# Layer 1's attention of a two-layer Perceiver: weights made key-major instead of query-major

## The chip, the cores and the metric

The kernel runs on one NeuronCore of a Trainium2 chip. The core has five instruction queues that run side by side and meet through semaphores: TensorE (PE in the profile, with PEld for its weight loads), VectorE (DVE), ScalarE (ACT), GpSimd (POOL) and SyncE (SP), which issues most of the DMAs. The metric is the device time of one execution in microseconds. Before the change it was 2016.11 us, the median of three runs (2011.85 to 2018.19).

## The reference, cut to what matters

A batch of 64 sequences of 32 tokens (2048 rows of 256 channels) passes two layers. Layer 0: attention over a context of 257 rows a sequence, an RWKV-like mixing with a feed-forward part, and a mixture of eight experts of which two are used. Layer 1: a second attention over the same context, a Mamba-like state-space recurrence, and a dense mixture of eight experts. Each part is added to the residual stream `x`.

The change lies in layer 1's attention alone. Queries, keys and values come from projections with ternary weights on quantised rows (the quantised context is kept in DRAM and is common to both). There are 16 query heads and 8 key/value heads of 16 channels; two query heads share a key head. For each sequence, head and query:

```python
w = softmax(q @ k.T)          # over 257 keys
o = w @ v                     # then a layer norm, a quantised output projection, and x + o
```

The softmax is computed as exponentials of the score less the row's maximum, divided by their sum.

## The kernel before, in words

The rows are worked in four blocks of 512 (16 sequences); a tile is 128 rows, four sequences, so there are 16 tiles. `_stage0` to `_stage5` build the two layers, and `layers` (L1294) writes them in program order, interleaving calls: layer-1 attention `s3` runs in slices of units while other stages' blocks are called between them. The order on each engine's queue is not that order by itself: the framework's scheduler places instructions by its own estimates, so the work of several stages is mixed on each queue, and each queue then runs strictly in the placed order.

A unit, `step` (L732), is two of a tile's four sequences. There are 32, two a tile. The work of a unit is spread over two steps: in the first, `keys` (L854) makes `kT` (PE L859, DVE L861) and `v` (PE L866, four ACT copies L874), and `scores` (L876), once for each pair of key heads, makes 128 queries x 256 keys of scores for two sequences in two PSUM banks (L882), their maxima on DVE (L887, joined with the score of the 257th key at L889), and eight exponentials a unit on ACT (L893), each with a sum along the row. In the next step `sums` (L898) turns these weights with 16 PE transposes (L911), copies them out on ACT (L913), multiplies them with the values (L919), and combines the two key heads that share a lane (ACT L924, DVE L925). After a tile's second unit `back` (L927) forms the reciprocals, brings them to the layout of the output with a small matmul, transposes the output, scales it, and adds the part of the 257th key (L931 to L967). After every second tile `finish` (L768) norms and quantises, and one step later projects and adds to `x` (L798).

`attend` (L802) opens a tile: it loads the quantised context and its steps, and makes the queries twice masked by `half` in `qm` (L840), the 257th key `klm` (L831) and value `vr` (L827), and the scores of that key (L843).

PSUM: pool `ps` has two banks with one tag; scores, `pt_ps` and more go through them. `pk` takes the one bank of `psp` where `k.lent` is set, else `ps`; while `k.idle` is set, `oT_ps` takes the bank of `psu`.

What follows from a block of layer-1 attention: `ahead` (L1023) norms `x` of a finished block, projects, convolves and makes the step sizes; then `recur` (L1087) begins with `dtx` (L1096) and runs 64 scans on DVE (L1110, with a product at L1111), each fed by an ACT exponential (L1109) and POOL products (L1105, L1116). After it come `head` and the experts of `_stage5` (L1265, L1273), a long run of 512-column matmuls.

## Time and profile before

| | |
|---|---|
| median of three runs | 2016.11 us |
| profiled execution, first to last instruction (span) | 2007.7 us; the profile gives no other time of it |
| median less span | 8.4 us |
| units 0 to 8 (start of unit 0's `kT` to unit 9's) | 490.9 to 779.6 us |
| recurrence 0, `dtx` and scans | 775.6, 780.9 to 998 us |
| recurrence 1 | 1088.2, 1096.8 to 1336 us |
| recurrence 2 | 1389.3, 1399.1 to 1635 us |
| last unit's combine (L925) | 1551.7 us |
| recurrence 3 | 1654.8, 1667 to 1843 us |
| the experts' rest, PE alone | 1843 to 2004 us |

How to read it. Each engine's share is a mean over stages with different limits, so a stretch is read by its own busy times. Busy PE time includes the pipelined end of each matmul, so PE that is busy all the time is not at its peak rate; how far matmuls are apart is read from their start times. "DVE L925" means a VectorE instruction of source line 925. In groups of instructions, the numbers after the bar are total busy us, mean ns of one, then idle us of the engine just ahead of these and what ended most of it.

### The profile page before, as it was taken

What the parts mean: (1) busy time and instruction counts of PE and PEld (TensorE: products, weight loads), DVE (VectorE), ACT (ScalarE), POOL (GpSimd) and SP (SyncE); (2) the same over time, 40 slices, a digit from 0 to 9 for tenths busy, and PEclk for the clock granted to TensorE, in tenths of its full rate; (3) what the DMA queues carried; (4) which work ended last, traced back from release to release, by engine and by line L of the source; (5) the groups of instructions that cost most, each with busy time, mean ns of one, the idle gap of its engine ahead of it and who ended that gap; (6) DMA issues with size and microseconds to landing.
All of it is one profiled execution on the core that took longest, in us unless ns stands there. A gap on an engine that the chain in (4) does not pass through costs nothing. (4 is left out here: it accounts for less than half of the span.)

```text
span 2007.7 us, 20180 instructions
## 1 busy us (share of the span) xinstructions
PE 1550.7 (77%) x6323; PEld 803.3 (40%) x6323; DVE 1272.7 (63%) x2207; ACT 999.6 (50%) x2172; POOL 1105.5 (55%) x1369
## 2 busy tenths in 40 slices
PE   4765966749988978766777878679878576898998
PEld 2333533424644633433443434334434233334443
DVE  4578477376385257988954778665768564876300
ACT  2453353121553436545537657548757454675432
POOL 5444655433134234777862578764678756998000
PEclk9686876769998989777787778779879796899999
DMA  7654324030000101222201223201313120442221
GB/s 228 218 182 146 119 94 127 26 102 0 22 22 22 53 11 59 64 53 64 74 11 49 64 52 106 74 32 49 106 42 85 59 63 21 125 126 64 74 84 42
DMA packets 88378, 151.25 MB, mean 75 GB/s; under 512 B 7740, under 2 KB 52300, under 8 KB 86224
## 3 DMA queue, kind: packets, MB, share of 16 engines
q1 hardware_dynamic: 85428, 148.75, 24.4%
q10 hardware_dynamic: 2844, 1.22, 0.3%
q8 instruction: 50, 0.82, 0.2%
q14 instruction: 56, 0.46, 0.1%
HBM read 139.03 MB, written 10.92 MB: 75 GB/s over the span
## 5 line engine op out<-in xcount | busy, mean ns | idle before, releaser
L1105 POOL TENSOR_TENSOR g<-dtx,bc 128x1024 f32<-128x1024 f32 x128 | 301.6, 2358 | 128.2 <-DVE h L1110 85.1
L1110 DVE TENSOR_TENSOR_SCAN h<-h,g 128x512 f32<-128x512 f32 x256 | 307.9, 1219 | 62.7 <-ACT h L1109 61.9
L1116 POOL TENSOR_TENSOR xc<-xc,hc 128x1024 f32<-128x1024 f32 x128 | 301.8, 2359 | 33.1 <-DVE hc L1111 26.7
L1265 PE MATMUL up<-xT,w 128*128 128x512 f32 x512 | 273.6, 655 | 20.5 <-ACT hid L1267 19.6
L1273 PE MATMUL acc<-hid,w 128*128 128x512 f32 x512 | 262.2, 637 | 28.4 <-ACT hid L1269 28.4
L1109 ACT ACTIVATE h<-dt,A 128x512 f32<-128x512 f32 x256 | 173.5, 693 | 98.9 <-DVE hc L1111 98.4
L1111 DVE TENSOR_TENSOR hc<-h,bc 128x512 f32<-128x512 f32 x256 | 170.8, 681 | 3.5
L893 ACT ACTIVATE p<-sc,nm 128x256 f32<-128x256 f32 x256 | 117.7, 471 | 111.1 <-DVE nm L889 100.3
L1273 PEld LDWEIGHTS acc<-hid,w 128*128 128x128 f32 x512 | 100.6, 205 | 148.1 <-issue 104.2
L1267 ACT ACTIVATE hid<-up,chan 128x512 f32<-128x512 f32 x128 | 86.7, 683 | 136.8 <-PE up L1265 136.6
L630 PE MATMUL weps<-we,xT 128*128 128x512 f32 x256 | 139.6, 672 | 19.2 <-DVE x L632 14.2
L1265 PEld LDWEIGHTS up<-xT,w 128*128 128x128 f32 x512 | 100.0, 207 | 132.9 <-issue 92.6
L882 PE MATMUL sc<-kT,qm 32*128 32x256 f32 x512 | 118.2, 449 | 7.4 <-ACT p L893 2.4
L911 PE MATMUL pt_ps<-ident,p 128*128 128x128 f32 x512 | 92.1, 315 | 30.1 <-ACT p L893 29.9
L887 DVE TENSOR_REDUCE nm<-sc 128x2 f32<-128x512 f32 x128 | 84.1, 684 | 28.2 <-PE sc L882 27.3
L911 PEld LDWEIGHTS pt_ps<-ident,p 128*128 128x128 f32 x512 | 64.8, 158 | 70.9 <-ACT p L893 48.9
L913 ACT COPY pt<-pt_ps 128x512 f32<-128x512 f32 x128 | 72.6, 586 | 38.9 <-PE pt_ps L911 31.4
L247 POOL TENSOR_TENSOR cT<-cT,scb 128x2056 f32<-128x2056 f32 x16 | 74.5, 4654 | 29.8 <-PE sc L258 11.1
L882 PEld LDWEIGHTS sc<-kT,qm 32*128 32x128 f32 x512 | 69.0, 205 | 45.7 <-issue 17.0
L1020 PE MATMUL inps<-xT,w_L_attn_in_projT 128*128 128x512 f32 x128 | 70.8, 679 | 20.6 <-ACT zs L1085 15.5
L919 PE MATMUL oT_ps<-pt,v 128*32 128x128 f32 x1024 | 68.8, 302 | 21.5 <-ACT pt L913 21.0
L530 POOL TENSOR_TENSOR kk<-kk 128x512 f32<-128x512 f32 x32 | 34.2, 1073 | 92.7 <-ACT kk L529 92.7
(407 smaller groups left out, 3032.7 us busy)
## 6 DMA issues: line engine op xcount, KB each, us to landing
bc<-rows SPq DMA_DIRECT2D x64, 512.0 KB
w<-in_L_ffn_w_dram SPq DMA_DIRECT2D x64, 512.0 KB
cT<-in_ctxT_dram SPq DMA_DIRECT2D x16, 1028.0 KB
cq<-cq SPq DMA_DIRECT2D x32, 514.0 KB
cn<-in_ctx_dram SPq DMA_DIRECT2D x64, 256.0 KB
scb<-scales SPq DMA_DIRECT2D x16, 514.0 KB
kb<-steps SPq DMA_DIRECT2D x16, 514.0 KB
x<-in_x_dram SPq DMA_DIRECT2D x4, 512.0 KB
```

The source lines that it names most:

```text
L630: nc.tensor.matmul(ps, xT[:, c, r], we[:, c, e : e + 2, :], start=c == 0, stop=c == 1)
L882: nc.tensor.matmul(sc[h][:, f, :], qm[r, e + f].rearrange("p l n g -> p (l n g)"), kTs[e][r, f, :], start=True, stop=True,)
L893: nc.scalar.activation(w_[:, f, h - h0, :], sc[h][:, f, :], AF.Exp, bias=nm[:, e + f, h : h + 1], accum_out=sm[:, e + f, h : h + 1],)
L911: nc.tensor.transpose(pt_ps[:, h, m, :], ws[e, hp][:, f, h, m * P : (m + 1) * P], k.ident)
L1105: nc.gpsimd.tensor_tensor(g, dtx[:, c2 : c2 + 2], bc[:, 0:1, :].to_broadcast([P, 2, BT]), ALU.mult)
L1109: nc.scalar.activation(h, dt, AF.Exp, scale=A[:, c2 + c, n : n + 1])
L1110: nc.vector.tensor_tensor_scan(h, h, g[:, c, :], 0.0, ALU.mult, ALU.add)
L1111: nc.vector.tensor_tensor(hc[:, c, :], h, bc[:, 1, :], ALU.mult)
L1116: nc.gpsimd.tensor_tensor(y[:, c2 : c2 + 2], y[:, c2 : c2 + 2], hc, ALU.add)
L1265: nc.tensor.matmul(u, w1[e][:, c, q * P : (q + 1) * P], xT[:, c, :], start=c == 0, stop=c == 1)
L1267: nc.scalar.activation(hid[e][:, q, :], u, AF.Identity, bias=b1)
L1273: nc.tensor.matmul(acc[o], w2[e][:, q, o * P : (o + 1) * P], hid[e][:, q, :], start=n == H, stop=n == E * H + H - 1)
```

## The change

The weights are made with keys along the partitions, the layout that the product with the values takes; the transposes of the weights go.

`tops` is the former `scores` without exponentials: the natural scores are made for their maxima only, and the negated maxima are written into a fixed tile `nmx`. `turn` transposes that tile once a unit (`nmT`), and makes the weights of the 257th key in turned form (`plT`). `weights`, in the next step, fills a PSUM bank a head with the negated maxima (a matmul that picks the row of the head and sequence and repeats it over all keys), adds keys times queries to it, and takes one exponential of 128x512 a head. `sums` multiplies with values laid out beside columns of ones (`vm`, `vls`), so that each product brings its weights' sum along with it; `back` transposes four 128x128 blocks, takes the reciprocals of the sums and multiplies. `values` is split from `keys` and moved to the end of the step, `qm` gets a second buffer, and the 257th key's values are made for 16 rows from a repeated copy on POOL (`ends4`). The scores are therefore computed twice, once in each layout.

```diff
--- before
+++ after
@@ -322,7 +323,8 @@

         of(dql, aml, ssl, "l")
         nc.scalar.dma_start(k.steps[:, :, 2 * P : S].rearrange("g e o -> (g e) o"), dql)
-        nc.sync.dma_start(k.dql, k.steps[:, :, 2 * P : S].rearrange("g e o -> e (g o)"))
+        for h in range(4):
+            nc.sync.dma_start(k.dql[4 * h : 4 * h + 4], k.steps[:, :, 2 * P : S].rearrange("g e o -> e (g o)"))
         cdq = k.cdq.rearrange("p t g -> p (t g)")
         of(cdq, am.rearrange("p t g -> p (t g)"), ss.rearrange("p t g -> p (t g)"), "s")
         dT_ps = pb.tile([P, P], F32, name="dT_ps", tag="b")
@@ -681,14 +683,40 @@
     half = w.tile([P, 2], F32, name="half", tag="half")
     nc.vector.tensor_reduce(half, k.ident.rearrange("p (i l d) -> p l i d", l=2, d=16), AX.XY, ALU.add)

-    sel = w.tile([P, T], F32, name="sel", tag="sel")
-    nc.vector.tensor_reduce(sel, k.ident.rearrange("p (l n g) -> p n l g", l=2, g=2), AX.XY, ALU.add)
-    lgm = w.tile([P, 2, 2], F32, name="lgm", tag="lgm")
-    nc.vector.tensor_reduce(lgm, k.ident.rearrange("p (l n g) -> p l g n", l=2, g=2), AX.X, ALU.add)
-    lgm = lgm.rearrange("p l g -> p (l g)")
-
...
+    three = w.tile([P, 3], F32, name="three", tag="three")
+    nc.vector.tensor_reduce(three, k.ident.rearrange("p (h r) -> p r h", r=32)[:, 0:3], AX.X, ALU.add)
+    pick = w.tile([P, 2, P], F32, name="pick", tag="pick")
+    nc.vector.tensor_copy(pick, three[:, 0:2].unsqueeze(2).to_broadcast([P, 2, P]))
+    pickl = w.tile([P, 4, 4, 4], F32, name="pickl", tag="pickl")
+    for e in range(4):
+        for at in range(4):
+            r = e % 2 if at == e else 2
+            nc.vector.tensor_scalar(pickl[:, e, :, at], k.bmask, three[:, r : r + 1], None, ALU.mult)
+
...
+    def fixed(name, shape, fill, rows=P):
+        t = k.wk3.tile([rows, *shape], F32, name=name, tag=name, bufs=1)
+        nc.gpsimd.memset(t, fill)
+        return t
+
+    nmxs = [fixed(f"nmx{n}", [4, 32], 0.0) for n in range(2)]
+    for nmx in nmxs:
+        nc.gpsimd.memset(nmx[:, :, 2:3], NONE)
+    klxs = [fixed(f"klx{n}", [68], 0.0) for n in range(2)]
+    vm = fixed("vm", [2, 2, 4, 2, 2, 16], 1.0)
+    vls = [k.wk3.tile([16, 2, 4, 2, 16], F32, name=f"vl{n}", tag=f"vl{n}", bufs=1) for n in range(2)]
+    for vl in vls:
+        nc.vector.tensor_copy(vl[:, :, :, 1, :], own.unsqueeze(1).unsqueeze(3).to_broadcast([16, 2, 4, 16]))
+    cdq = w.tile([P, 8, NT], F32, name="cdq3", tag="cdq3")
+    nc.vector.tensor_scalar(cdq, k.cdq, mw[:, 2:3], None, ALU.mult)
+    dql1 = w.tile([16, NT], F32, name="dql1", tag="dql1")
+    nc.vector.tensor_scalar(dql1, k.dql, mw[0:16, 2:3], None, ALU.mult)
+    dql = w.tile([16, NT, 4], F32, name="dql3", tag="dql3")
+    nc.vector.tensor_tensor(
+        dql, own.unsqueeze(1).to_broadcast([16, NT, 4]), dql1.unsqueeze(2).to_broadcast([16, NT, 4]), ALU.mult,
+    )

...
@@ -742,12 +770,19 @@
                 h = halves[t // 2]
                 tiles[t] = attend(t, t % 2, h.xq, h.dq, h.o4)
             tiles[t].keys(e)
-            tiles[t].scores(e, 0)
+            tiles[t].tops(e, 0)
         if old:
             lt, le = divmod(2 * u - 2, 4)
+            tiles[lt].weights(le, 0)
+        if new:
+            tiles[t].tops(e, 2)
+        if old:
+            tiles[lt].weights(le, 2)
+        if old:
             tiles[lt].sums(le)
         if new:
-            tiles[t].scores(e, 2)
+            tiles[t].turn(e)
+            tiles[t].values(e)
         if old and le == 2:
             tiles[lt].back()
             if lt % 2:
@@ -819,37 +854,46 @@
         nc.scalar.activation(q, q_ps, AF.Copy, scale=dq[:, j : j + 1])

         last_ps = pk([P, P + 4], "last_ps")
+        ends4 = k.small.tile([P, 2, 4, 4], BF16, name="ends4", tag="ends4")
         for c in range(2):
-            nc.tensor.matmul(last_ps[0:4, 0:P], cq[:, c, :, 2 * P], wkv[:, c, P : 2 * P], start=c == 0, stop=c == 1)
+            nc.gpsimd.tensor_copy(ends4[:, c], cq[:, c, :, 2 * P].unsqueeze(1).to_broadcast([P, 4, 4]))
+        for c in range(2):
+            nc.tensor.matmul(
+                last_ps[0:16, 0:P], ends4[:, c].rearrange("p h e -> p (h e)"), wkv[:, c, P : 2 * P],
+                start=c == 0, stop=c == 1,
+            )
         for c in range(2):
             nc.tensor.matmul(last_ps[:, P : P + 4], wkv[:, c, 0:P], cq[:, c, :, 2 * P], start=c == 0, stop=c == 1)
-        vr = k.wk3.tile([4, P], F32, name="vr", tag="vr")
-        nc.scalar.activation(vr, last_ps[0:4, 0:P], AF.Copy, scale=k.dql[:, g : g + 1])
+        klx, vl = klxs[g % 2], vls[g % 2]
+        nc.vector.tensor_tensor(
+            vl[:, :, :, 0, :], last_ps[0:16, 0:P].rearrange("p (h l d) -> p l h d", l=2, d=16),
+            dql[:, g].unsqueeze(1).unsqueeze(3).to_broadcast([16, 2, 4, 16]), ALU.mult,
+        )
         kl = last_ps[:, P : P + 4]
         nc.vector.tensor_tensor(kl, kl, kb[:, :, 2 * P], ALU.mult)
-        klm = k.small.tile([P, 4, 4], F32, name="klm", tag="klm")
         nc.vector.tensor_tensor(
-            klm, kl.unsqueeze(2).to_broadcast([P, 4, 4]), k.bmask.unsqueeze(1).to_broadcast([P, 4, 4]), ALU.mult
+            klx.rearrange("p (e q) -> p e q", q=17)[:, :, 0:16].rearrange("p e (h m) -> p e h m", m=4)[:, :, :, 0],
+            kl.unsqueeze(2).to_broadcast([P, 4, 4]), k.bmask.unsqueeze(1).to_broadcast([P, 4, 4]), ALU.mult,
         )
+        klx = klx[:, 0:64].rearrange("p (e h m) -> p e h m", h=4, m=4)
...
-        qm = k.wk3.tile([P, 4, 2, T, 2], F32, name="qm", tag="qm", bufs=1)
+        qm = k.wk3.tile([P, 4, 2, T, 2], F32, name="qm", tag="qm")
         for l in range(2):
             nc.scalar.activation(qm[:, :, l].rearrange("p e n g -> p g e n"), qT_ps, AF.Copy, scale=half[:, l : l + 1])
         sl_ps = pk([P, 4, 4], "sl_ps")
         for e in range(4):
-            nc.tensor.matmul(sl_ps[:, e, :], qm[:, e].rearrange("p l n g -> p (l n g)"), klm[:, e, :], start=True, stop=True)
+            nc.tensor.matmul(sl_ps[:, e, :], qm[:, e].rearrange("p l n g -> p (l n g)"), klx[:, e, :, e], start=True, stop=True)
         nsl = k.small.tile([P, 4, 4], F32, name="nsl", tag="nsl")
         nc.scalar.activation(nsl, sl_ps, AF.Copy, scale=-1.0)

...
@@ -859,6 +903,8 @@
                 nc.tensor.matmul(kT_ps, wkv[:, c, 0:P], cq[:, c, e : e + 2, 0 : 2 * P], start=c == 0, stop=c == 1)
             kTs[e] = k.wk3.tile([P, 2, 2 * P], F32, name="kT", tag="kT")
             nc.vector.tensor_tensor(kTs[e], kT_ps, kb[:, e : e + 2, 0 : 2 * P], ALU.mult)
+        def values(e):
+
             v_ps = pk([P, 2, 2, P], "v_ps")
             for m in range(2):
                 for f in range(2):
@@ -867,13 +913,15 @@
                             v_ps[:, m, f, :], cq[:, c, e + f, m * P : (m + 1) * P], wkv[:, c, P : 2 * P],
                             start=c == 0, stop=c == 1,
                         )
-            vs[e] = k.wk3.tile([P, 2, 2, P], F32, name="v", tag="v")
-            cd = k.cdq[:, :, g].rearrange("p (m e) -> p m e", m=2)[:, :, e : e + 2]
+            cd = cdq[:, :, g].rearrange("p (m e) -> p m e", m=2)[:, :, e : e + 2]
             for m in range(2):
                 for f in range(2):
-                    nc.scalar.activation(vs[e][:, m, f, :], v_ps[:, m, f, :], AF.Copy, scale=cd[:, m, f : f + 1])
-
-        def scores(e, h0):
+                    nc.scalar.activation(
+                        vm[:, m, f, :, :, 0, :], v_ps[:, m, f, :].rearrange("p (h l d) -> p h l d", l=2, d=16),
+                        AF.Copy, scale=cd[:, m, f : f + 1],
+                    )
+
+        def tops(e, h0):
             hs = range(h0, h0 + 2)
             sc = {h: ps([P, 2, 2 * P], "sc") for h in hs}
             for f in range(2):
@@ -885,15 +933,49 @@
                     )
             for h in hs:
                 nc.vector.tensor_reduce(nm[:, e : e + 2, h], sc[h], AX.X, ALU.max, negate=True)
-            n2 = nm[:, e : e + 2, h0 : h0 + 2]
-            nc.vector.tensor_tensor(n2, n2, nsl[:, e : e + 2, h0 : h0 + 2], ALU.min)
-            w_ = ws[e, h0 // 2] = k.wk3.tile([P, 2, 2, 2 * P], F32, name="p", tag="p", bufs=3)
+            nmx[e] = nmxs[(2 * g + e // 2) % 2]
+            nc.vector.tensor_tensor(
+                nmx[e][:, h0 : h0 + 2, 0:2].rearrange("p h f -> p f h"),
+                nm[:, e : e + 2, h0 : h0 + 2], nsl[:, e : e + 2, h0 : h0 + 2], ALU.min,
+            )
+
+        def turn(e):
+
+            nl_ps = pk([P, 3, P], "nl_ps")
+            nc.tensor.transpose(nl_ps[:, 2, :], nmx[e].rearrange("p h r -> p (h r)"), k.ident)
+            nmT[e] = k.wk3.tile([P, P], F32, name="nmT", tag="nmT", bufs=1)
+            nc.scalar.copy(nmT[e], nl_ps[:, 2, :])
+            for f in range(2):
+                o = nl_ps[0:16, f, :]
+                nc.tensor.matmul(o, pickl[:, e + f].rearrange("p h m -> p (h m)"), nmT[e], start=True, stop=False)
+                nc.tensor.matmul(
+                    o, klx[:, e + f].rearrange("p h m -> p (h m)"), qm[:, e + f].rearrange("p l n g -> p (l n g)"),
+                    start=False, stop=True,
+                )
+            plT[e] = k.wk3.tile([16, 2, P], F32, name="plT", tag="plT", bufs=1)
+            nc.scalar.activation(plT[e], nl_ps[0:16, 0:2, :], AF.Exp)
+
+        def weights(e, h0):
+            hs = range(h0, h0 + 2)
+            sT = {h: ps([P, 2, 2, P], "sT") for h in hs}
+            for f in range(2):
+                for h in hs:
+                    r = slice(32 * h, 32 * h + 32)
+                    nc.tensor.matmul(
+                        sT[h][:, f], pick[r, f, :], nmT[e][r, :].unsqueeze(1).to_broadcast([32, 2, P]),
+                        start=f == 0, stop=False, skip_group_check=True,
+                    )
+            for f in range(2):
+                for m in range(2):
+                    for h in hs:
+                        r = slice(32 * h, 32 * h + 32)
+                        nc.tensor.matmul(
+                            sT[h][:, f, m, :], kTs[e][r, f, m * P : (m + 1) * P],
+                            qm[r, e + f].rearrange("p l n g -> p (l n g)"), start=False, stop=True, skip_group_check=True,
+                        )
             for h in hs:
-                for f in range(2):
-                    nc.scalar.activation(
-                        w_[:, f, h - h0, :], sc[h][:, f, :], AF.Exp, bias=nm[:, e + f, h : h + 1],
-                        accum_out=sm[:, e + f, h : h + 1],
-                    )
+                ws[e, h] = k.wk3.tile([P, 2, 2, P], F32, name="p", tag="p", bufs=4)
+                nc.scalar.activation(ws[e, h], sT[h], AF.Exp)

         def sums(e):

@@ -902,71 +984,38 @@
             else:
                 oT_ps = pk([P, 2, 2, 2 * T], "oT_ps")
             for f in range(2):
-                pts = []
-                for hp in range(2):
-
-                    pt_ps = ps([P, 2, 2, P], "pt_ps")
-                    for h in range(2):
-                        for m in range(2):
-                            nc.tensor.transpose(pt_ps[:, h, m, :], ws[e, hp][:, f, h, m * P : (m + 1) * P], k.ident)
-                    pt = k.wk3.tile([P, 2, 2, P], F32, name="pt", tag="pt")
-                    nc.scalar.copy(pt, pt_ps)
-                    pts.append(pt)
-                ob = oT_ps[:, f].rearrange("p l q -> p (l q)")
+                for l in range(2):
+                    nc.tensor.matmul(
+                        oT_ps[:, f, l, :], vls[g % 2][:, l].rearrange("p h w d -> p (h w d)"),
+                        plT[e][:, f, l * 2 * T : (l + 1) * 2 * T], start=f == 0 and l == 0, stop=False, skip_group_check=True,
+                    )
+            for f in range(2):
                 for m in range(2):
-                    for h in range(4):
-                        r = slice(32 * h, 32 * h + 32)
-                        nc.tensor.matmul(
-                            ob[r], vs[e][:, m, f, r], pts[h // 2][:, h % 2, m, :],
-                            start=m == 0, stop=m == 1, skip_group_check=True,
-                        )
-            o2 = od4[:, e : e + 2]
-            nc.scalar.activation(o2, oT_ps[:, :, 0], AF.Copy, scale=half[:, 0:1])
-            nc.vector.scalar_tensor_tensor(o2, oT_ps[:, :, 1], half[:, 1:2], o2, ALU.mult, ALU.add)
+                    for l in range(2):
+                        for h in range(4):
+                            nc.tensor.matmul(
+                                oT_ps[32 * h : 32 * h + 32, f, l, :], vm[:, m, f, h, l].rearrange("p w d -> p (w d)"),
+                                ws[e, h][:, f, m, l * 2 * T : (l + 1) * 2 * T], start=False, stop=m == 1, skip_group_check=True,
+                            )
+            nc.scalar.copy(
+                od.rearrange("p l (e n) g -> p e l (n g)", e=4)[:, e : e + 2], oT_ps,
+            )

         def back():

-            rp = k.small.tile([P, 2, 4, 4], F32, name="rp", tag="rp3", bufs=1)
-            rs, pl = rp[:, 0], rp[:, 1]
-            nc.vector.tensor_tensor(pl, nm, nsl, ALU.subtract)
-            nc.scalar.activation(pl, pl, AF.Exp)
-            nc.vector.tensor_tensor(sm, sm, pl, ALU.add)
-            nc.vector.reciprocal(rs, sm)
-            nc.vector.tensor_tensor(pl, pl, rs, ALU.mult)
-
...
-            o = o4[:, j].rearrange("p i l g d -> p g (i l) d")
-            nc.vector.tensor_tensor(o, po_ps, over(0), ALU.mult)
...
-            nc.gpsimd.tensor_tensor(o, o, t, ALU.add)
-
-        a.keys, a.scores, a.sums, a.back = keys, scores, sums, back
+
+        a.keys, a.values, a.tops, a.turn, a.weights, a.sums, a.back = keys, values, tops, turn, weights, sums, back
         return a

     return run
```

## The prediction

> **What bounds the kernel now.** I read the page first, then the busy time of each engine stretch by stretch, cut at the starts of units (a unit is one step of the layer-1 attention, two of a tile's four sequences; there are 32).
>
> ```profile
> span 2007.7 us, 20180 instructions
> PE 1550.7 (77%) x6323; PEld 803.3 (40%) x6323; DVE 1272.7 (63%) x2207; ACT 999.6 (50%) x2172; POOL 1105.5 (55%) x1369
> ...
> L893 ACT ACTIVATE p<-sc,nm 128x256 f32<-128x256 f32 x256 | 117.7, 471 | 111.1 <-DVE nm L889 100.3
> ...
> L911 PE MATMUL pt_ps<-ident,p 128*128 128x128 f32 x512 | 92.1, 315 | 30.1 <-ACT p L893 29.9
> L887 DVE TENSOR_REDUCE nm<-sc 128x2 f32<-128x512 f32 x128 | 84.1, 684 | 28.2 <-PE sc L882 27.3
> ...
> L913 ACT COPY pt<-pt_ps 128x512 f32<-128x512 f32 x128 | 72.6, 586 | 38.9 <-PE pt_ps L911 31.4
> ...
> L919 PE MATMUL oT_ps<-pt,v 128*32 128x128 f32 x1024 | 68.8, 302 | 21.5 <-ACT pt L913 21.0
> ```
>
> No engine is full over the span; the groups that change wait for one another in a ring, DVE maxima, ACT exponentials, PE transposes, ACT copies, PE sums. Which wait costs depends on the stretch (time of units 0-8, 9-13, 14-18, 19-23, 24-26, 27-31):
>
> ```profile
> 490.90:779.60 288.70, 256.88 (x1234) 145.12 (x1232) 152.00 (x349) 141.05 (x354) 89.45 (x209) 0.92 0.09 27
> 779.60:933.70 154.10, 107.67 (x560) 59.85 (x559) 141.44 (x234) 78.22 (x208) 117.79 (x112) 0.77 0.20 55
> 933.70:1075.90 142.20, 107.83 (x570) 56.83 (x569) 104.73 (x205) 73.95 (x193) 89.69 (x153) 0.83 0.15 47
> 1075.90:1250.00 174.10, 136.80 (x600) 70.73 (x601) 127.16 (x196) 114.39 (x246) 114.49 (x97) 0.79 0.26 72
> 1250.00:1404.50 154.50, 122.34 (x472) 60.09 (x472) 95.93 (x148) 96.15 (x176) 99.51 (x126) 0.86 0.18 56
> 1404.50:1552.00 147.50, 117.96 (x632) 62.65 (x629) 118.58 (x190) 97.39 (x227) 109.64 (x95) 0.87 0.26 76
> ```
>
> After start, end and length stand PE, PEld, DVE, ACT, POOL, then the granted clock. Units 0-8 lean on PE; 9-13 are full on DVE (141.44 of 154.10), which also runs the scans of the state-space recurrence (L1110, L1111). Later nothing is full: two chains alternate, the units of a block and then that block's recurrence. Inside the first stretch, by 20 us:
>
> ```profile
> 520.00:540.00 20.00, 20.00 (x108) 12.61 (x106) 5.46 (x15) 10.70 (x34) 3.54 (x4) 1.00 0.00 1
> 560.00:580.00 20.00, 19.74 (x97) 10.25 (x95) 16.11 (x36) 14.10 (x33) 9.70 (x17) 1.00 0.01 2
> 580.00:600.00 20.00, 13.07 (x60) 6.90 (x58) 18.96 (x26) 10.37 (x23) 5.96 (x4) 0.83 0.00 0
> 660.00:680.00 20.00, 20.00 (x119) 12.32 (x118) 6.02 (x13) 9.86 (x32) 4.01 (x7) 1.00 0.24 81
> ```
>
> PE never rests in most slices; in 580-600 the layer-0 scan fills DVE instead. Rates come from the timeline's starts:
>
> ```profile
> 533.29 1.51 PE L882 MATMUL sc<-kT,qm 32*128 32x256 f32 x8
> 540.22 0.63 PE L919 MATMUL oT_ps<-pt,v 128*32 128x128 f32 x12
> 540.78 0.66 PE L911 MATMUL pt_ps<-ident,p 128*128 128x128 f32 x4
> ```
>
> At clock 1.00 two `sc` records in two row groups start every 0.215 us, transposes every 0.11, four `oT` records in four column groups every 0.107. (An fp32 matmul is two records, a transpose one.)
>
> **The change per unit.**
> PE. Removed: 16 transposes x 0.11 = 1.76 and 32 sums records / 4 x 0.107 = 0.86, together 2.6. Added: `weights`, 16 records of 256 columns in pairs, 8 x 0.215 = 1.72, and 32 of 128 columns in pairs, 16 x 0.11 = 1.76; `turn`, 9 x 0.11 = 1.0; `sums`, 8 for the last key x 0.11 = 0.9 and 64 in fours, 16 slots between 0.055 (half the columns) and 0.107, I take 0.08 = 1.3. Together 6.6, net **+4.0 us of PE a unit** (+3.5 to +6; the top if key records cannot pair). 32 units: +128 us of PE.
> ACT. Exponentials follow one another every 0.449 (activate plus accumulator read), copies of 128x512 every 0.477: 8 x 0.449 + 4 x 0.477 + 0.27 = 5.8. New: 4 exponentials of 128x512, nearest row L1109 (0.625 apart), 2.5, and copies of 128x128 and 128x256 and one small exponential near 0.3 each, 0.9. **-2.4 us**; between -3 and -1.8 if reading PSUM or the strided rows of `vm` is dearer.
> DVE. The combine L925 goes (0.344). Per tile L931-L938, L962 and L966 took 54.7/16 = 3.4 us, since some small ones were stretched up to 2 us beside POOL; reciprocal, product and `vl` cost 0.25 + 0.43 + 0.2 by L934, L962, L829. **-1.6 us a unit.**
> POOL: an add of 0.73 a tile goes, two 16-element copies (about 0.2 each by L785) come. `last_ps` on PE now waits for those copies behind POOL's 2.36 us products; with `qT` and `sl` queued behind it. It is hidden by work placed before it; uncovered, 16 tiles x at most 2.4 = 38, kept in the range. SP gets three more `dql` loads and DVE/POOL some 30 set-up instructions ahead of unit 0, together +1 (0 to +4). Tiling-mode changes (start distance 0.31 instead of 0.215 where `cv` gives way to `oT`) rise from 409 to 451 by the built order, 42 x 0.09 = 4 us spread over the kernel, costed at nothing under other idle.
> The chain of one lone unit, by the rows with 0.1 per handover: before kT 1.4, twice score, maxima, exponentials 4.4, four transpose-and-copy pairs 3.5, sums and combine 1.6, values 1.8, half a tile's start 2.2, 19; after kT 1.4, twice tops 2.6, twice weights 3.4, sums 2.8, turn 2.4, values 1.8, 2.2, **23 us**. The PSUM pair gets fewer handovers, but turn and double weights are longer. New waits on PE: `turn`'s eight matmuls wait for the ACT copy `nmT`, with `v_ps` and the next unit's `kT_ps` behind them; each `sT` group waits until both maxima have emptied the two banks, with fill work of the other stages behind it. Both are in the 23. `values` moves from behind `kT` to behind `turn`: its 8 matmuls and 4 ACT copies no longer stand ahead of the scores, and go into one `vm` that the sums before must have read, which they have by their place.
>
> At one place a rule is to be weighed. In the first `sc` burst the loads of two row groups start at 533.674 and 533.680, 6 ns apart, so loads pair and I use 0.11 a pair. The Trainium skill, "TensorE: Matmul & The Clock Gate", section "LDWEIGHTS (loading the stationary operand)", says a load's time goes by its columns, 32 rows costing what 128 do, 128 columns about 107 ns. Should the key loads run singly at that figure, a unit would cost 1.7 us more and by an estimate from it the sum would be 15 us higher.
>
> **Where it lands.** The built order shows that the planner now packs more scans between units: between unit 9 and 14 all 64 of recurrence 0 (43 before), then none until unit 19. I added each unit's DVE instructions in that order, times row medians (L1110 and L1111 by their spacing, 1.13 and 0.61). Before, units 9-13 hold 133 us and took 154 (0.86); 19-23 116 in 174 (0.67); 27-30 84 in 113 (0.75). After: 163, 155 and, for 27-31, about 150.
> 1. Units 0-8: 8 x 4.0 = 32 us, of which 13 of 24 ten-us slices are PE-full, 17; stalls inside them take a third: **+12** (0 to +45).
> 2. Recurrence 0 (779.6) to the `dtx` of recurrence 1 (1088.2), 308.6: five dense units 163/0.86 = 189, 3.5 lone ones x 23 = 81, block out to `dtx` 54 as now: 324, **+15** (-20 with 0.95 and 19 us; +51 with 0.80 and 28).
> 3. To `dtx` of recurrence 2 (1389.3), 301.1: 144/0.80 = 180 (between 0.67 and 0.86, as ACT is freer), 1.5 x 23 = 35, out to `dtx` 60 (54 without a recurrence beside it, 78 now): 275, **-26** (-58 to +28).
> 4. To `dtx` of recurrence 3 (1654.8), 265.5: 150/0.80 = 187, last sums 10, finish 28, out to `dtx` 57: 282, **+16** (-13 to +71).
> 5. Tail: at the end of the attention 14 expert matmuls fewer are done, 14 x 0.86 = 12 us; PE idles 23 of 100 us until 1843, so a third is felt: **+4** (-5 to +15).
> With set-up 1 the sum is **+22**: span 2030, and 2016 + 22 = **2038** in the median's terms; the profiled span lies 8.4 below the median, what lies around it unchanged.
>
> **Rivals.**
> A, faster: freed ACT keeps DVE fed in the dense stretches. For: ACT waits 100.3 us for `nm` and DVE's port-stretched operations go. Against: the planner's bunching leaves DVE idle from unit 14 to 18. The dense lists sum to 457 us; my 556 us of time are a mean 0.82, and 22 less is 0.856: from there on it is faster. At 0.92 the dense stretches give -59, six lone units at 21 give -12, with +22 that is -49, 1967; typically half of it, **1991**.
> B, PE takes the bound: key records unpaired and fill work stuck behind `sT`. Lone units 28 (six x 5 = +30), first stretch +45 in place of +12, tail +15: +22 + 74, **2112** at the end, typically 2085. Against it: at the full rate all PE work from 480 to 2000 is only 933 us by the timeline's records.
> C, no change: the terms of both signs cancel, **2016**.
>
> **Chances.** Forecast (slower by 0.3 to 2.5%) 0.41; B 0.15; A 0.36; C 0.08, C being what 0.3% of the median, 6 us, cannot tell from nothing. The likeliest case alone: 2024 to 2062. The range takes in most of A and B and leaves out about one in ten on each side: 1970 to 2100.
>
> **What will show it.** PE near 8800 records; `sT` groups of 12 matmuls in about 1.8 us (over 2.6: loads don't pair); exponentials near 0.69; units 9 to 14 at 35 us or more with DVE over 0.9 busy, and 14 to 18 near 23 with DVE half idle. The prediction is wrong if units 9-18 fit in less than 270 us, if units 0-8 take no longer than 289, or if recurrence 3 starts before 1667 less 15.

## The result, and the profile after

The changed kernel took 2146.01 us (median of 4 runs, 2138.54 to 2153.22) against 2013.98 us of the kernel before on the same chip (2008.89 to 2018.19): a ratio of 1.066, with a 95% interval of 1.062 to 1.069. It is slower by 132 us. The forecast was 2038 with a range up to 2100: the direction held, the size was six times too small.

The page of the kernel after, the totals and the groups of the attention (busy us, mean ns of one, then the idle time just ahead and what ended it):

```profile
span 2144.2 us, 24576 instructions
PE 1760.4 (82%) x8787; PEld 1002.6 (47%) x8787; DVE 1233.1 (58%) x2132; ACT 888.9 (41%) x1673; POOL 1104.5 (52%) x1392
...
L964 PE MATMUL sT<-nmT,pick 32*128 32x256 f32 x512 | 145.2, 551 | 60.1 <-DVE nm L935 59.5
L978 ACT ACTIVATE p<-sT 128x512 f32<-128x512 f32 x128 | 69.2, 591 | 179.0 <-PE sT L972 178.9
L972 PE MATMUL sT<-qm,kT 32*128 32x128 f32 x1024 | 132.9, 360 | 0.0
L930 PE MATMUL sc<-kT,qm 32*128 32x256 f32 x512 | 103.4, 505 | 28.5 <-DVE kT L905 12.8
```

ACT and DVE were relieved as meant, ACT by 111 us and DVE by 40. PE got 210 us more of busy time. The place where ACT waited has moved: before, its exponentials stood 100.3 us for DVE's maxima; now they stand 178.9 us for PE's `sT`, and PE itself stands 59.5 us for the maxima ahead of the picks. This last wait is new.

The busy time by stretch, cut at the starts of units 0, 9, 14, 19, 24, 27, at the end of the scans of recurrence 2, at the `dtx` of recurrence 3, and late in the tail (start and end, length, PE, PEld, DVE, ACT, POOL, granted clock, DMA share, GB/s):

```profile
488.10:814.60 326.50, 299.47 (x1855) 189.55 (x1854) 143.27 (x320) 109.19 (x213) 86.37 (x211) 0.85 0.08 24
814.60:1005.10 190.50, 148.96 (x935) 100.18 (x935) 170.43 (x255) 76.69 (x153) 167.87 (x139) 0.66 0.21 56
1005.10:1166.80 161.70, 141.49 (x963) 85.73 (x963) 64.45 (x155) 46.38 (x97) 40.67 (x131) 0.82 0.11 35
1166.80:1389.60 222.80, 178.08 (x1030) 109.25 (x1030) 171.53 (x237) 112.29 (x193) 177.60 (x136) 0.76 0.24 64
1389.60:1511.90 122.30, 109.34 (x628) 59.27 (x626) 40.38 (x87) 61.14 (x96) 32.61 (x92) 0.86 0.13 38
1511.90:1700.00 188.10, 160.42 (x949) 97.03 (x949) 150.77 (x210) 88.13 (x156) 153.82 (x113) 0.66 0.24 68
1700.00:1793.20 93.20, 76.26 (x304) 40.38 (x302) 30.52 (x80) 44.28 (x62) 40.56 (x112) 0.87 0.15 43
1793.20:1980.00 186.80, 155.71 (x369) 69.71 (x369) 140.19 (x223) 118.64 (x144) 161.81 (x76) 0.94 0.34 96
```

Two kinds of stretch alternate. In the dense ones (second, fourth, sixth) the scans share the time with the units: DVE is 0.77 to 0.89 busy and the granted clock of PE falls to 0.66 to 0.76. In the third and fifth the units run without scans: DVE is 0.40 and 0.33 busy, PE 0.88 and 0.89. There PE is the engine with the least room, though it stands for DVE at times, too (the row at 1050 below). Against the forecast's segments (times of the span, before to after):

| segment | before | after | forecast | measured |
|---|---|---|---|---|
| to the `dtx` of recurrence 0 | 775.6 | 815.6 | +12 (and +1 set-up) | +40 |
| to that of recurrence 1 | 312.6 | 362.0 | +15 | +49 |
| to that of recurrence 2 | 301.1 | 325.8 | -26 | +25 |
| to that of recurrence 3 | 265.5 | 289.8 | +16 | +24 |
| to the end | 352.9 | 351.0 | +4 | -2 |

Rows of the timeline show how one and the same burst of 24 records (eight picks, sixteen keys; it is made 64 times) runs with a warm PE (granted clock 1.00) and a cold one (0.50), and what two of the cold ones stood behind (start, length, engine and line; idle time before in brackets):

```profile
506.58 1.29 PE L964 MATMUL sT<-nmT,pick 32*128 32x256 f32 x6 [0.77 <-DVE nm L935]
507.94 1.26 PE L972 MATMUL sT<-qm,kT 32*128 32x128 f32 x13
...
604.62 2.24 PE L964 MATMUL sT<-nmT,pick 32*128 32x256 f32 x7 [5.23 <-DVE nm L935]
606.70 2.30 PE L972 MATMUL sT<-qm,kT 32*128 32x128 f32 x15
...
1042.55 2.27 DVE L116 TENSOR_SCALAR xe<-xe,mv,rstd 128x256 f32<-128x256 f32 x4 [3.99 <-POOL rstd L93]
1046.80 0.43 DVE L102 BATCH_NORM_STATS2 st<-x 128x6 f32<-128x256 f32 x1 [1.64 <-POOL x L1187]
1049.31 1.27 DVE L935 TENSOR_REDUCE nm<-sc 128x2 f32<-128x512 f32 x2
1050.04 2.24 PE L964 MATMUL sT<-nmT,pick 32*128 32x256 f32 x7 [6.97 <-DVE nm L935]
```

After a pause of 0.77 us the burst took 2.62 us from its first start to its last end; after 5.23 us it took 4.38. At 1042 the scores had been ready (their last record ends at 1041.8), but DVE's queue held a norm that waited for POOL ahead of the reductions; so PE stood for 6.97 us, with other stages' matmuls behind the picks, and then ran cold. Over the 57 bursts that no other record interrupts the mean was 3.78 us: 21 ran at a clock of 1.00 and took 2.06 to 2.62, 32 ran at 0.50 and took 3.79 or more. These three bursts by the windows, and a later stretch (in the order of the table above):

```profile
506.58:509.20 2.62, 2.62 (x25) 2.41 (x25) 0.71 (x2) 0.17 (x1) 0.00 (x0) 1.00 0.23 86
604.62:609.00 4.38, 4.38 (x25) 4.05 (x25) 2.87 (x8) 1.23 (x5) 3.11 (x5) 0.50 0.00 0
1050.04:1054.41 4.37, 4.37 (x25) 4.04 (x26) 1.62 (x6) 0.32 (x1) 2.58 (x13) 0.50 0.00 0
509.60:526.70 17.10, 17.10 (x116) 9.69 (x115) 1.46 (x3) 3.13 (x8) 1.04 (x1) 0.50 0.00 1
```

The Trainium skill, "TensorE: Matmul & The Clock Gate", in "Part 1: The HAM clock gate", says that an idle window of about 3.4 us halves the clock and that a busy window of this length restores it. The pauses of 0.77, 5.23 and 6.97 us ahead of these three bursts agree with the first half of this. The second half does not hold in the last of the four windows: from 509.60 to 526.70 PE was busy throughout, and the clock stayed at 0.50, so that here the measurement decides. Nor does the pause just ahead tell how most bursts run: of the 32 at 0.50, 27 stand behind less than 3.4 us of idle time, ten of them behind none. The whole kernel idles PE for less time than before (384 us for 457) and has the lower mean clock (0.810 for 0.845), so longer pauses alone are not what lowered it; what else did, no run here separates. The forecast priced these bursts at full clock.

### The profile page after: what moved, and what is told of

The parts are those of the page before. It is cut to its first block, busy times and chain, and to the rows that moved or that the text cites. A ratio compares the mean times of both kernels' runs of the same rounds, so it can differ in the third digit from the quotient of the medians.

```text
span 2144.2 us, 24576 instructions
## 1 busy us (share of the span) xinstructions
PE 1760.4 (82%) x8787; PEld 1002.6 (47%) x8787; DVE 1233.1 (58%) x2132; ACT 888.9 (41%) x1673; POOL 1104.5 (52%) x1392
## 5 line engine op out<-in xcount | busy, mean ns | idle before, releaser
L1322 PE MATMUL acc<-hid,w 128*128 128x512 f32 x512 | 266.8, 641 | 18.4 <-ACT hid L1318 18.4
L964 PE MATMUL sT<-nmT,pick 32*128 32x256 f32 x512 | 145.2, 551 | 60.1 <-DVE nm L935 59.5
L964 PEld LDWEIGHTS sT<-nmT,pick 32*128 32x128 f32 x512 | 90.4, 257 | 117.5 <-DVE nm L935 98.8
L978 ACT ACTIVATE p<-sT 128x512 f32<-128x512 f32 x128 | 69.2, 591 | 179.0 <-PE sT L972 178.9
L972 PEld LDWEIGHTS sT<-qm,kT 32*128 32x128 f32 x1024 | 132.1, 269 | 7.0 <-issue 2.4
L972 PE MATMUL sT<-qm,kT 32*128 32x128 f32 x1024 | 132.9, 360 | 0.0
L930 PE MATMUL sc<-kT,qm 32*128 32x256 f32 x512 | 103.4, 505 | 28.5 <-DVE kT L905 12.8
L930 PEld LDWEIGHTS sc<-kT,qm 32*128 32x128 f32 x512 | 61.9, 236 | 86.4 <-ACT p L978 25.2
L1336 DVE SCALAR_TENSOR_TENSOR last<-rT,gt,x 128x256 f32<-128x256 f32 x16 | 7.1, 476 | 149.8 <-PE rT L1335 149.6
L634 DVE SCALAR_TENSOR_TENSOR x<-weps,pr,x 128x256 f32<-128x256 f32 x128 | 60.9, 476 | 51.6 <-PE weps L632 50.5
```

The lines of the kernel that those rows point to most:

```text
L930: nc.tensor.matmul(sc[h][:, f, :], qm[r, e + f].rearrange("p l n g -> p (l n g)"), kTs[e][r, f, :], start=True, stop=True,)
L964: nc.tensor.matmul(sT[h][:, f], pick[r, f, :], nmT[e][r, :].unsqueeze(1).to_broadcast([32, 2, P]), start=f == 0, stop=False, skip_group_ch ...
L972: nc.tensor.matmul(sT[h][:, f, m, :], kTs[e][r, f, m * P : (m + 1) * P], qm[r, e + f].rearrange("p l n g -> p (l n g)"), start=False, stop ...
L1322: nc.tensor.matmul(acc[o], w2[e][:, q, o * P : (o + 1) * P], hid[e][:, q, :], start=n == H, stop=n == E * H + H - 1)
```

## Experiments

Two theories stood first. The work theory: the added PE time itself, inside the unit's ring, is what costs. The wait theory: the loss is PE standing for DVE's maxima before it may fill a bank. A warm us below is a us of PE time at full clock by the spacing of starts, over all 32 units. The kernel before was run beside each group of experiments, with medians of 2012.4 to 2017.5 us; a ratio goes by the one beside it, and differences between runs of different groups, as those to the 2146.01 of the kernel after, carry some 5 us from that.

**Scores made three times (on the kernel before).** 16 more records of 256 columns twice over, 3.4 us a unit, 110 us.

```diff
-            for f in range(2):
+            for f in [f for _ in range(3) for f in range(2)]:
```

> The kernel before with each score matmul made three times into the same bank: +3.4 us of PE a unit at the warm rate (16 records, eight pairs of 0.215, twice more), nearly the +4.0 of the change, without a second use of the banks and with no other engine's work touched. Work theory (the change costs the time of its added matmuls, which push other stages' matmuls back): 2095 to 2125 us. Wait theory (the added matmuls fit into idle PE time; what costs is that the turned scores stand in PE's queue until VectorE has emptied the two score banks): 2015 to 2050 us.

Measured 2196.68, ratio 1.089 (1.087 to 1.092), +179 us on the 2017.49 of before on that chip. PE work put into the ring, with no new wait for anything, costs 1.6 us per warm us, dearer than even the work theory held. The occupied time of the scores (each record to the next start, or its own end) grew from 113 to 244 us, 131 for 110; the other 48 of the 179 us are not the matmuls' own time.

**No picks, maxima over the keys, and these with picks twice (on the kernel after).** The first takes out 55 warm us and leaves the wait; the second takes out the score matmuls (55 warm us) and with them the wait for the banks; the third puts the same PE work back without the wait.

```diff
-                    nc.tensor.matmul(
-                        sT[h][:, f], pick[r, f, :], nmT[e][r, :].unsqueeze(1).to_broadcast([32, 2, P]),
```
```diff
-                nc.vector.tensor_reduce(nm[:, e : e + 2, h], sc[h], AX.X, ALU.max, negate=True)
+                nc.vector.tensor_reduce(nm[:, e : e + 2, h], kTs[e], AX.X, ALU.max, negate=True)
```
```diff
+                    nc.tensor.matmul(
+                        sT[h][:, f], pick[r, f, :], k.ident[r, (32 * h + 64) % P : (32 * h + 64) % P + 1]...,
```

> The changed kernel without the matmuls that add the negated maxima (the weights of the 256 keys are then exponentials of the plain scores while the last key's keeps its maximum, so the sums are of mixed scale): -1.7 us of PE a unit, all waits kept. Work theory: 55 to 65 us less than the changed kernel, about 2088. Wait theory: at most 25 less, 2120 to 2145.

> The changed kernel without the natural scores: VectorE takes its maxima over the keys in SBUF instead (same size and count, other numbers, so the weights are scaled otherwise). PE has 1.7 us less a unit, as without the picks, but here no bank waits for VectorE's maxima any more. Work theory: the same as without the picks, about 2088. Wait theory: 2020 to 2050, 70 or more below the run without the picks.

> As the run with maxima over the keys, but the pick matmuls are made a second time with zeros as moving operand, so PE has as many matmuls and the same columns as the changed kernel; only the wait of the banks for VectorE is gone. Work theory: 2130 to 2160 as the changed kernel. Wait theory: 2040 to 2085.

Measured 2044.05 (ratio 1.013, 1.010 to 1.017), 2035.36 (1.009, 1.007 to 1.011) and 2108.18 (1.045, 1.043 to 1.047). Without picks PE's wait for the maxima is still there (59.5 us in the kernel after):

```profile
PE sT L965 <- DVE nm L935: 52.4, 30, 7.2
```

and yet 102 us are won, more than the work theory's 55 to 65. This contradicts the wait theory. The second run alone would have supported it (-111 us, in the range of the wait theory, though only 9 and not 70 below the run without picks), but it takes out matmuls as well as the wait. The third separates them, and falls between the ranges of both theories: with as many matmuls as the kernel after, and no wait, 38 us are won. So the wait, with the maxima no longer standing behind the scores, is worth some 38 of the 132 us, and the second set of picks 73 (2108 - 2035).

**Matmuls that nobody reads (before), and the units in another order (after).** If PE were simply full, work beside the ring would cost as much as work in it. 3.4 warm us a unit of 512-column matmuls go into a PSUM tile that nobody reads (it takes its turn in `ps`, or in the bank of `psp`, as other tiles do); in the other run the old unit's `weights` and `sums` are written ahead of the new unit's keys and scores.

```diff
+            idle_ps = pk([P, 512], "idle_ps")
+            for n in range(4):
+                nc.tensor.matmul(idle_ps, k.ident, beta.unsqueeze(1).to_broadcast([P, 2, D]), start=True, stop=True)
```
```diff
-            tiles[t].keys(e)
-            tiles[t].tops(e, 0)
...
             tiles[lt].weights(le, 0)
...
             tiles[lt].sums(le)
         if new:
+            tiles[t].keys(e)
+            tiles[t].tops(e, 0)
+            tiles[t].tops(e, 2)
```

> The kernel before with four more fp32 matmuls of 512 columns a unit (8 x 0.43 = 3.4 us of PE at the warm rate, as much as the two further rounds of score matmuls), on constants and into a bank that nobody reads, so no step of a unit waits for them. Ring theory (the units are a closed ring of PE, VectorE and ScalarE steps that sets the pace, so a matmul costs what it adds inside the ring, at the granted clock): clearly less than the 179 us of the tripled scores, 2015 to 2090. Load theory (PE as a whole is short of time, wherever the matmuls stand): again +150 to +190, 2165 to 2205.

> The changed kernel with another order of the step: both weights and the sums of the old unit first, then keys, both tops and the turn of the new one, so that only one of the two turned score groups stands behind a maximum. Matmuls and all other work are unchanged. Ring theory: the ring is as long as before, 2125 to 2170. Wait theory (the rest of the 38 us that the wait was worth): 2100 to 2125. A planner that fills better either way could shift it by 20.

Measured 2070.35 (ratio 1.027, 1.025 to 1.029): +55 us, as the ring theory has it, a third of what the same warm time cost in the ring. These matmuls differ from the scores in form, too (128 rows and 512 columns for 32 and 256), and scores made beside the ring were not tried, so place and form are not separated here. And 2138.51 (1.059, 1.056 to 1.063), some 8 us under the kernel after: this other order is worth little, and is not the cause. The page with the unread matmuls:

```profile
span 2067.5 us, 20722 instructions
PE 1637.2 (79%) x6579; PEld 833.4 (40%) x6579; DVE 1282.5 (62%) x2207; ACT 1001.3 (48%) x2170; POOL 1108.1 (54%) x1369
...
L754 PE MATMUL idle_ps<-beta,ident 128*128 128x512 f32 x256 | 130.3, 652 | 11.6 <-DVE od L929 6.4
```

PE stood 11.6 us ahead of them, 6.4 of it for DVE's `od`. They were occupied 126 us, while PE's total rose by 86 only (1551 to 1637): the rest of PE's work became 40 us shorter, at a mean granted clock of 0.863 in place of 0.845.

**No maxima at all, in both kernels.** From the kernel after go `tops`, the picks and the turning of the maxima; from the kernel before go the reductions and the bias of the exponentials.

```diff
-            tiles[t].tops(e, 0)
...
-            tiles[t].tops(e, 2)
```
```diff
-                        w_[:, f, h - h0, :], sc[h][:, f, :], AF.Exp, bias=nm[:, e + f, h : h + 1],
+                        w_[:, f, h - h0, :], sc[h][:, f, :], AF.Exp,
```

> The changed kernel without maxima at all: no natural scores, no picks, no turning of the maxima; the turned weights are exponentials of the plain scores (the softmax is the same as long as nothing overflows). If the three terms measured so far add up (-102 picks, -73 score matmuls at the price of the zero picks, -38 the wait): 1920 to 1950 us, faster than the kernel before. If they overlap, since another chain takes over: 1960 to 2010.

> The kernel before without maxima: exponentials of the plain scores, no VectorE reduction (4 x 0.6 and two small ones, 2.9 us a unit), PE's work as before. Ring theory: the maxima are a serial part of every unit, about 32 x 2.9 = 93 less, 1915 to 1950. Load theory: VectorE counts only where it is full, the ten units of the first recurrence, 10 x 2.9: 1985 to 2000. Against the changed kernel without maxima it tells which layout is better when neither needs the second scores.

Measured 1995.66 (ratio 0.989, 0.986 to 0.993) and 2003.77 (0.994, 0.992 to 0.996). The first is 150 us under the kernel after, not the 213 that the two separate removals would add up to. The second fell far short of the ring theory, though recurrence 3 began 55 us sooner: its last scan came 43 us sooner, and from there to the end it took 203 us in place of 166. The same is seen in the first, by its windows from the last scan on and those of the kernel before:

```profile
1771.80:1996.00 224.20, 214.65 (x534) 99.35 (x534) 22.50 (x109) 73.74 (x81) 10.10 (x18) 0.98 0.21 66
```
```profile
1841.60:2004.00 162.40, 152.78 (x390) 71.51 (x388) 22.51 (x108) 52.75 (x58) 11.49 (x18) 0.98 0.19 59
```

The last scan comes 70 us earlier, but PE then works alone for 62 us longer. Of the experts' 1024 matmul records 562 were done by the last scan in the first run and 622 in the second, 707 before. So the shorter units had less expert work done beside them, and the tail takes that back.

**Exponentials twice (before).** The same length into the ring, 3.6 us a unit or 115 us, but on ACT.

```diff
-                for f in range(2):
+                for f in [0, 1, 0, 1]:
                     nc.scalar.activation(
```

> The kernel before with each of the eight exponentials of a unit done twice (the second writes the same again): 8 x 0.449 = 3.6 us more of ACT a unit, inside the ring, no work for PE. It puts the same warm time into the ring as the thrice-made scores did on PE (3.4 us a unit, +179). Theory of length (any engine's time inside the ring costs the same, because it lengthens the ring): +120 to +190, 2135 to 2205. Theory of PE (the price is that of an engine on which other stages' work is queued behind the ring's matmuls, and of its clock; ACT is idle half the time and lengthens the ring only where nothing else is the bound): +10 to +80, 2025 to 2095.

Measured 2114.09 (ratio 1.050, 1.047 to 1.053), +102 us. It lies below the theory of length and above that of PE: a ring that is longer on an engine with idle time costs 0.9 per us.

```profile
span 2119.4 us, 20669 instructions
PE 1618.5 (76%) x6323; PEld 840.7 (40%) x6323; DVE 1271.4 (60%) x2207; ACT 1118.5 (53%) x2686; POOL 1110.9 (52%) x1369
```

PE has the same 6323 records as before, and is busy for 1618.5 us in place of 1550.7, at a granted clock of 0.807 in place of 0.845. So part of the price of a longer ring is paid by PE's own work.

**Stage 1 earlier.** In the kernel after, the last matmuls of stage 1 ran behind the units of block 0. Its last two calls are written ahead of unit 4.

```diff
-        s3(0, 8, first=True, last=True)
+        s3(0, 4, first=True)
         s1(NBLK - 2)
         s1(NBLK - 1)
+        s3(4, 8, last=True)
```

> The kernel after with the last two calls of stage 1 written ahead of unit 4 instead of behind unit 7, nothing else changed. Theory of displaced fill (28 of the 40 us lost ahead of recurrence 0 are stage-1 matmuls that the planner put behind the longer units): recurrence 0's dtx comes 15 to 28 us earlier than 815.6, total 2115 to 2135. Theory of the full engine (PE has no room in this stretch whatever the order, the 40 us are the added PE time itself): dtx stays within 8 us of 815.6, total 2135 to 2155.

> The kernel after without maxima (the weights are then exponentials of the bare scores, the shift by the row's maximum is left out), and with stage 1 earlier as in the run beside it. Displaced fill: 10 to 25 us less than the 1996 of the kernel without maxima, 1970 to 1985, if the recurrences' tail does not take it back. Full engine: 1990 to 2002.

> The kernel before with the last two calls of stage 1 ahead of unit 4. The same edit gave +17 us on the kernel after (2163 against 2146) and -54 on the kernel after without maxima (1942 against 1996). Theory of the order alone (the edit pays wherever PE is not full in units 0 to 8; the -54 have nothing to do with the maxima): recurrence 0's dtx 10 to 25 us ahead of 775.6, total 1960 to 1995. Theory of room (it pays only where the units are as short as without maxima; with maxima the units' own rings set the end): dtx no sooner than 770, total 2005 to 2030.

On the kernel after: 2162.94 (ratio 1.074, 1.073 to 1.076), 17 us more. Without maxima: 1941.58 (0.963, 0.960 to 0.966), 54 us less, the fastest version here. On the kernel before: 2056.41 (1.021, 1.016 to 1.025), 40 us more. None of these was expected; the traces suggest why. From the end of attention block 0 (where its last two tiles begin to be added to `x`) to the `dtx` of recurrence 0 it took 57 us before, 85 in the kernel after and 160 without maxima. Stage 1's last matmul ended at 699.5 us before, at 749.5 in the kernel after and at 730.8 without maxima, against block ends of 718.8, 730.6 and 632.7. Stage 1 was clearly the last to be ready in the third, and only there does moving it forward help (`dtx` at 771.5, not 792.5; the rest is won in later segments, 22 us of it ahead of recurrence 3, by what was not looked into). Before, the units were late, and the same move puts them behind stage 1 (`dtx` at 823.0, not 775.6; all later segments together change by 1 us). In the kernel after, between the two, the move ends stage 1 at 683.6 and block 0 only at 778.0, and `dtx` moves from 815.6 to 830.4. That is argued from these times and not tried by itself. So "displaced fill" was no loss that this move could win back: PE was busy 83.8 of the 88 us from 728 to 816, and the work moved out of there made the units late instead.

**Other doses.** Since each variant is placed anew by the scheduler and one move of two calls was worth from -54 to +40 us, it had to be seen whether the prices above are prices or scatter. Scores twice, eight unread matmuls, exponentials three times (all on before), and a second set of picks on the kernel after.

```diff
-            for f in [f for _ in range(3) for f in range(2)]:
+            for f in [f for _ in range(2) for f in range(2)]:
```
```diff
-            for n in range(4):
+            for n in range(8):
```
```diff
-                for f in [0, 1, 0, 1]:
+                for f in [0, 1, 0, 1, 0, 1]:
```

> The kernel before with its score matmuls made twice: half the dose of the thrice-made ones (+179 us for 110 us of warm PE time). Theory of a price by work in the ring: half of it, +65 to +115. Theory of the order (the planner places everything anew for each variant, and the same small move of two calls was worth +41, +17 and -54 us on three kernels; what was put down to work is its scatter): no relation to the dose, anywhere from -30 to +180, so that outside +65 to +115 it gains.

> The kernel before with eight matmuls a unit that nobody reads in place of four: twice the dose of the run that gave +55 us for 110 us of warm PE time off the ring. Price by work: twice that or more, since less idle time is left to take it, +95 to +170. Order: no relation to the dose.

> The kernel before with each exponential three times: twice the dose of the run that gave +102 us for 115 us of ACT time in the ring. Price by work: +180 to +260. Order: no relation to the dose.

> The kernel after with a second set of picks that adds zeros: 55 us more of warm PE time in the ring, which took 73 us where they were added to the kernel with the maxima over the keys and gave 102 us where they were taken out of the kernel after. Price by work: +65 to +110 over after, 2205 to 2255. Order: no relation.

Measured 2095.93 (ratio 1.044, 1.039 to 1.048), 2164.87 (1.075, 1.072 to 1.078), 2223.48 (1.104, 1.102 to 1.107) and 2249.95 (1.118, 1.115 to 1.120; 104 us over the kernel after), against 2014.43 of before. All four lie in the bands of the price.

| added (us over before, by the medians, if nothing else is said) | full-rate us | cost, us | per us |
|---|---|---|---|
| scores twice, three times: PE in the ring | 55, 110 | +82, +179 | 1.5, 1.6 |
| picks: added to the maxima over keys; added to after; taken out of after | 55 | 73, 104, 102 | 1.3, 1.9, 1.9 |
| exponentials twice, three times: ACT in the ring | 115, 230 | +102, +209 | 0.9, 0.9 |
| unread matmuls, four, eight: PE beside the ring | 110, 220 | +55, +150 | 0.5, 0.7 |

With the exponentials three times, PE's 6323 records take longer still, and the clock is 0.796:

```profile
PE 1636.3 (74%) x6323; PEld 848.7 (38%) x6323; DVE 1276.3 (57%) x2207; ACT 1230.3 (55%) x3195; POOL 1106.0 (50%) x1369
```

## Why the prediction was wrong

**The net +4.0 us of PE a unit was mis-sized.** The instruction counts were right (8787 records, about 8800 forecast), the rates were those of a warm PE in the middle of a burst. The forecast's own row at 533.29 has eight `sc` records in 1.51 us at a clock of 1.00, where four pairs of 0.215 make 0.86. By occupied time, the groups that went (scores, transposes and sums before) held 254 us and those that came (`sT` 231, scores 99, sums 96.5, `turn` 44) hold 470: 6.75 us a unit more, at the clocks that they had. An `sT` group, worked out at 1.74 us and announced as "about 1.8", takes 2.1 to 2.6 warm, with its pipelined end, and 3.78 on the mean. The forecast read "over 2.6: loads don't pair" into such a time; that test was badly chosen. The loads do pair: in the burst at 506.58 key records start 1786 and 1787, 1897 and 1899, 2009 and 2011 ns behind its first, and in the warm bursts the sixteen lie within 0.82 to 1.38 us from first start to last, where fifteen steps of 107 ns would make 1.6. So rival B's first cause is denied. The 107 ns for 128 columns are those of the Trainium skill ("TensorE: Matmul & The Clock Gate", "LDWEIGHTS (loading the stationary operand)"); the case that the forecast left open, such loads one behind another, did not come about. It is the clock, and the ends of bursts, that lengthen them.

**What PE time costs was mis-priced most.** The forecast's terms give 22 us for 128 us of added PE time and the relief of ACT and DVE together; it counted on PE's idle time and wrote against rival B that all PE work is only 933 us at the full rate. The runs say 1.3 to 1.9 per us in the ring. As a rough estimate by the table: 128 x 1.6 = 205; less ACT's 2.4 us x 32 at 0.9, 69; plus 38 for the wait, 174 (143 with the 111 us by which ACT's busy time fell), of which DVE's relief takes a little. 132 was measured; the prices do not add up exactly, as the removals did not (102 + 111 against 150).

Term by term:

1. Units 0 to 8, +12 forecast, +40. Block 0 itself was right (its end came 12 us later, 718.8 to 730.6); the other 28 came between it and `dtx`, where stage 1 ran late (its last matmul at 749.5, not 699.5). The step that failed is the 13 of 24 slices and the third of the stalls, by which 20 of 32 us were to be absorbed: PE's busy time in units 0 to 8 rose by 42.6 us (256.9 to 299.5), its idle time fell by 5 only (31.8 to 27.0), and the stretch grew by 38.
2. +15 against +49. The dense units were right, 189 forecast and 190.5 measured; so was the mechanism, DVE 0.89 busy. The lone units were not: 111.5 us for 3.5, 32 each, where the row by row chain gave 23. This chain used warm bursts and a handover of 0.1; the waits of the row at 1050 (6.97 us behind another stage's norm on DVE) are in none of its rows. From block end to `dtx` it took 61, not 54.
3. -26 against +25, the one wrong sign. The dense part took 212 us to unit 24 where 144/0.80 = 180 was put: freed ACT hardly raised DVE's share (144/212 is 0.68 by the forecast's list, 0.67 before). The 1.5 lone units took 61, not 35; from there to `dtx` it took 53, as against 60.
4. +16 against +24; the block end to `dtx` took 58 (57 forecast). Of the right size.
5. +4 against -2: right, as a sum, by luck. From `dtx` to the last scan it took 30 us less, from there to the end 28 more; the forecast had neither.

**Rivals.** A (freed ACT keeps DVE fed) fell: the dense stretches ran at 0.89, 0.77 and 0.80 of DVE, with a clock of 0.66 to 0.76; by the forecast's lists 457 us of DVE work took some 596 us, 0.77, where A needed more than 0.856. B named the right engine and the right consequence, fill work stuck behind `sT`, and its lone unit of 28 was nearer than 23; its 2112 was still 34 us short. What decided in its favour is that PE work in the ring is paid more than once: as length, as cold clock for all of PE's work, and as a queue held up for other stages. The runs show the sum of these and, by the unchanged 6323 records, the second; the third is seen in single rows, as that at 1050. They do not divide it further.

**What was right of the signs.** ACT's and DVE's relief in direction (111 and 40 us of busy time, where 77 and 51 were put), `dtx` after block 3, units 9 to 14 at 38 us each. Exponentials took 0.591 us (0.69 was put). The set-up cost nothing that shows: unit 0 began at 488.1, not 490.9. Of the signs named for a wrong forecast, units 9 to 18 in less than 270 us, units 0 to 8 in no more than 289 and recurrence 3 before 1652, none came (352, 326.5, 1793): all three looked for an error to the fast side.

## What to carry to other kernels

Where units wait in a ring that no engine fills, price added work by where it stands and not by the engine's idle share: a warm us of PE cost 0.5 to 0.7 beside the ring (in matmuls of another form) and 1.3 to 1.9 inside it, and an idle engine's us inside it still 0.9. Take a burst's length from rows of whole bursts, first start to last end, at the clock that the stretch had, and not from the spacing inside a warm one. A version that computes a thing twice to spare a transpose must win more by what it spares than the second computation costs at such a price; here, leaving out the maxima altogether and then moving the late stage forward gave 1942 us, but it holds only while the scores stay small enough for bare exponentials.

## What the runs showed of the hardware that was not expected

Longer work on ACT made PE's unchanged work longer: 6323 records, 1550.7, 1618.5 and 1636.3 us busy with the exponentials once, twice and three times, at a granted clock of 0.845, 0.807 and 0.796. Matmuls that nobody reads did the reverse: 0.863 with four a unit, 0.869 with eight, and with four the rest of PE's work shrank by 40 us. It did not pay: the kernel was 55 us slower for them. And the clock does not go by PE's idle time alone: the kernel after idled PE for 384 us at 0.810, with picks twice for 365 us at 0.788, the kernel before for 457 us at 0.845. In the kernel after the clock stayed at 0.50 for 17 us (509.60 to 526.70) with PE busy throughout. The matmuls added there have 32 rows and those that nobody reads 128; whether that is the reason was not tried.
